# Attention scores moved from inside the gate to the expert tiles, and all DCT tiles of the next group into the gate

## The chip, the cores and the metric

The kernel runs on one core of one Trainium2 chip. The metric is the device time of one execution in microseconds (us). Engines are named TensorE (PE), VectorE (DVE), ScalarE (ACT), GpSimd (POOL) and SyncE (SP, which issues transfers).

## What is computed

64 audio signals of 80000 samples are cut into 157 frames of 512 samples. Everything is float32.

```
h = frames @ DCT.T                                   # per signal: 157 tokens x 512
x = layernorm(h)
key, query = exp(i*pi*tanh(x @ Wk)), exp(i*pi*tanh(x @ Wq))   # 4 sets x 8 planes
V = x @ Wv + bv
total = sum over sets and planes of Re(cumsum(key * V) * conj(query)), weighted
pos_contrib = the same with fixed positional phases
gate = sigmoid(x @ Wg + bg)
total = gate * total + (1 - gate) * pos_contrib
h = h + x + total / norm @ Wo + bo
x = layernorm(h)
scores = softmax(mean over tokens of x @ Wg_ffn + bg_ffn)     # 16 experts
e = argmax(scores)                                   # one expert per signal
h = h + scores[e] * (x @ We[e] + be[e])
```

The cumulative sums are computed as a causal matrix product: scores of query and key tokens, masked, then applied to V.

## The kernel before

The 64 signals are worked in 16 groups of 4. A group's 4 x 160 padded tokens make five tiles: four of 128 tokens (32 tokens of each of the 4 signals) numbered 0 to 3, and a tile called TAIL. The order of instructions is written out by hand; each engine works through its own list, and semaphores between engines are set from what each instruction reads and writes. TensorE's results go to PSUM through one pool of four buffers of two banks (`psum()`, L91), which every stage shares, so a stage may have to wait until an earlier result has been read out.

The main loop (L1218) does for each group g, after a special first group:

1. `project_and_values(g)` (L1085): query and key phases, V by seven products of half size (a Strassen-like scheme), and, for the group before, the turning of the normalised tokens (`x2T`), the choice of the expert (`route`, `pick`) and the fetch of its weights (`fetch`, four indirect transfers issued by POOL). Near its end stands `fold_twice(g+1, 0)`: DVE folds the first half of the next group's frames (`xT`) for the DCT.
2. `gate(g)` (L1133): seven gate products in the order 1, 6, 2, 7, 5, 4, 3 (`gate_product`, matmuls at L655), each followed by DVE sums of its result (L100) and ACT tanh operations (L672). Products 2, 4 and 3 go on adding in the buffers of products 1, 7 and 5. Between the products stand other steps: `fold_once` and `fold_twice(g+1, 1)` for the second half of the next frames, `scores(g)` and the DCT of the next group's tiles.
3. `experts_and_embedding(g)` (L1155): three of the five expert tiles of group g-1, the rest of the DCT tiles of group g+1, their layernorm factors, and the loads of group g+2's frames.
4. `attention(g)` (L1174): the scores are applied to V (`read`, L697), two more expert tiles (L1185, L1210) and the output products.

Group 15 has no next group: its gate does no DCT, and `experts_and_embedding` is left out. So `experts_and_embedding` runs for groups 1 to 14.

The steps that the change moves:

- `scores(g)` (L674): 20 matmuls of 32 columns each, L681, then two DVE operations (L682, L683) that make `att`, which `read` uses.
- `embed(g, n)` (L259) is the DCT of one tile: two matmuls at L270 and two at L272, on the folded frames. `embed_statistics` (L284) takes its result out of PSUM: two ACT copies (L292, L293), a DVE add and subtract (L294, L295), then layernorm moments on DVE (L232, L233). For tile 0 and 1 it needs the first half of the frames, for 2, 3 and TAIL the second half too.
- `embed_deviations` (L304): a few small POOL operations over the five tiles' moments; `embed_res` on ACT follows them.
- `expert(g, n)` (L960): 16 matmuls at L940 into the four 32-row strips of one buffer, one strip for each of the four signals with its own weights `we`; then `expert_out` (L948), one DVE operation (L951), and the stores to DRAM issued by SP.
- `add_bias(g, n)` (L931): one DVE operation (L934) per tile.
- `keep_deviations` and `spread_deviations` (L329, L337): the layernorm factors go to DRAM and come back to all partitions as `scale`, issued by SP; `scale_all` in `attention` uses them on DVE (L363).

Sums and differences on DVE that go through the helpers `add` and `sub` appear in the profile at L100 and L99, whoever calls them. A float32 matmul of the program is executed as two passes, so 16 expert matmuls appear as 32 in the profile.

Of the kernel before, what the change touches and what calls it, by code (L numbers as in the profile page):

```python
# [30 lines left out]
TAIL = NM - 1  # L31
# [22 lines left out]
def audio_tower(ctx: ExitStack, tc: tile.TileContext, a, out):  # L54
# [36 lines left out]
    def psum():  # L91

        return ps_mm.tile([P, 2, 512], F32, tag="mm", name="mm")

    def bank():
        return psum()[:, 0, :]
# [8 lines left out]
    def tile_of(x, n):  # L105
        return x[..., P * SLOT[n] : P * (SLOT[n] + 1)]
# [122 lines left out]
    def moments(mv, h):  # L229

        st = small.tile([P, 6], F32, tag="st", name="st", bufs=4)
        nc.vector.bn_stats(st, h)  # L232
        nc.vector.bn_aggr(mv, st)  # L233

    def deviation(rstd, var):

        nc.gpsimd.tensor_scalar(rstd, var, EPS, None, ALU.add)  # L237
        nc.gpsimd.tensor_tensor(rstd, rstd, power[:, : rstd.shape[-1]], ALU.pow)

    def shifts(mean, rstd):  # L240

        shift = small.tile([P, NM], F32, tag="shift", name="shift")[:, : rstd.shape[-1]]
        nc.gpsimd.tensor_tensor(shift, mean, rstd, ALU.mult)
        nc.gpsimd.tensor_scalar(shift, shift, -1.0, None, ALU.mult)  # L244
        return shift
# [13 lines left out]
    def embed(g, n):  # L259

        s = S[g]
        if n == 0:
            s["res"] = {}
            s["res2"] = []
        h = psum()
        h, odd = h[:, 0, :], h[:, 1, :].rearrange("p (n j) -> p n j", n=2)
        by_r = h.rearrange("p (j r) -> p r j", r=4)
        ft = tile_of(s["xT"], n)
        for i in range(2):
            nc.tensor.matmul(by_r[:, 2 * i, :], ft[:, 2 + i], dct_e[:, i, :], start=True, stop=True)  # L270
        for i in range(2):
            nc.tensor.matmul(odd[:, i, : P + 1], ft[:, i], trig_o[:, i, :], start=True, stop=True)  # L272
        s["h", n] = h, odd

    def residual(g, n):

        s = S[g]
        if n == TAIL:
            return p1.tile([P, D], F32, tag="res_t", name="res_t", bufs=3)
        if n % 2 == 0:  # L280
            s["res2"].append(p1.tile([P, 2, D], F32, tag="res", name="res", bufs=6))
        return s["res2"][-1][:, n % 2, :]

    def embed_statistics(g, n):  # L284
        s = S[g]
        if n == 0:
            s["mv"] = small.tile([P, NM, 2], F32, tag="mv", name="mv", bufs=2)
        h, odd = s.pop(("h", n))
        s["res"][n] = r = residual(g, n)
        of_r, to_r = (x.rearrange("p (j r) -> p r j", r=4) for x in (h, r))  # L290
        sines = p2.tile([P, P + 1], F32, tag="sines", name="sines")
        nc.scalar.copy(sines, odd[:, 1, : P + 1])  # L292
        nc.scalar.copy(to_r[:, 0::2, :], of_r[:, 0::2, :])  # L293
        add(to_r[:, 1, :], odd[:, 0, :P], sines[:, :P])  # L294
        sub(to_r[:, 3, :], odd[:, 0, 1 : P + 1], sines[:, 1 : P + 1])  # L295
        moments(s["mv"][:, SLOT[n], :], r)
# [7 lines left out]
    def embed_deviations(g, of=range(NM), known=False):  # L304

        s = S[g]
        lo, hi = min(SLOT[n] for n in of), max(SLOT[n] for n in of) + 1
        rstd, mv = deviations[g % 2][:, lo:hi], s["mv"][:, lo:hi]
        if not known:
            deviation(rstd, mv[:, :, 1])  # L310
        shift = shifts(mv[:, :, 0], rstd)
        more = small.tile([P, NM], F32, tag="more", name="more", bufs=6)[:, : hi - lo]
        nc.gpsimd.tensor_scalar(more, rstd, 1.0, None, ALU.add)  # L313
        for n in of:
            k = slice(SLOT[n] - lo, SLOT[n] - lo + 1)
            s["rstd", n] = rstd[:, k]
            s["st", n] = shift[:, k], more[:, k]
# [329 lines left out]
    def gate_product(g, i):  # L647

        s = S[g]
        if i == 1:  # L650
            s["gT"] = p1.tile([P, C, 2 * HN], F32, tag="gT", name="gT")
        (ps, first), rhs, w = room(g, i), operand(g, i), fac_g[i]
        for o in range(2):
            for c in range(2):
                nc.tensor.matmul(  # L655
                    ps[:, o, :HN],
                    w[:, c, o * P : (o + 1) * P],
                    rhs[:, c],
                    start=(first and c == 0),
                    stop=(c == 1),  # L660
                    skip_group_check=not first,
                )
        part = halves(s["gT"])
        if i != 2:
            gather(i, by_halves(ps), part)
        for k, m, n in ((2, 0, 0), (5, 1, 1), (3, 0, 1), (4, 1, 0)):
            if k == i:
                for o in range(2):
                    to = part[m][n][:, o]
                    c = 2 * n + o  # L670
                    of = ps[:, o, :HN] if i == 2 else to
                    nc.scalar.activation(to, of, AF.Tanh, bias=hbg[:, c : c + 1], scale=0.5)  # L672

    def scores(g):  # L674

        ps = bank()
        for n in range(NM):
            lo, hi = SEES[n]
            for i in range(GB):
                to = ps[Q * i : Q * (i + 1), START[n] : START[n] + hi - lo]  # L680
                nc.tensor.matmul(to, kf[:, SLOT[n], i], qf[:, lo // Q : hi // Q, i], start=True, stop=True)  # L681
        nc.vector.tensor_tensor(att[:, 0], ps[:, :NS], hmask, ALU.mult)  # L682
        nc.vector.tensor_tensor(att[:, 1], att[:, 0], share, ALU.add)  # L683
# [247 lines left out]
    def add_bias(g, n):  # L931

        s = S[g]
        nc.vector.scalar_tensor_tensor(s["res"][n], s["be"], s["gate"], s["res"][n], ALU.mult, ALU.add)  # L934

    def expert_chunk(g, n, c, ps):

        s = S[g]
        for i in range(GB):
            nc.tensor.matmul(  # L940
                ps[Q * i : Q * (i + 1), :],
                s["x2T"][:, c, i, Q * n : Q * (n + 1)],
                s["ws"][i][:, c, :],
                start=(c == 0),
                stop=(c == C - 1),
            )

    def expert_out(g, n, ps):  # L948
        s = S[g]
        o, at = s["res"][n], Q * BLOCK[n]  # L950
        nc.vector.scalar_tensor_tensor(o, ps, s["gate"], o, ALU.mult, ALU.add)  # L951
        for i in range(GB):

            for lo, hi in ((0, Q),) if n < TAIL else ((0, Q // 2), (Q // 2, LT)):
                queue = nc.sync if g + 1 < NG or i % 2 == 0 else nc.scalar
                if g + 2 == NG and n in ORDER[1:4]:
                    queue = nc.gpsimd
                queue.dma_start(out=out[GB * g + i, at + lo : at + hi, :], in_=o[Q * i + lo : Q * i + hi, :])

    def expert(g, n, between=lambda c: None):  # L960
        ps = psum()
        for c in range(C):
            between(c)
            expert_chunk(g, n, c, ps[:, 0, :])
        between(C)
        expert_out(g, n, ps[:, 0, :])
# [166 lines left out]
    def gate(g):  # L1133
        ahead = g + 1 < NG
        for i in (1, 6, 2, 7, 5, 4, 3):
            gate_product(g, i)
            if i == 1:
                pick_gate(g - 1)
                bias(g - 1)
                fold_once(g + 1, 1)  # L1140
                add_bv(g, 0, slice(H, D))
                add_bv(g, 1)
            elif i == 5:
                scores(g)
                fold_twice(g + 1, 1)
                if ahead:
                    embed(g + 1, 0)
                    embed_statistics(g + 1, 0)
            elif i == 4 and ahead:
                add_bias(g - 1, TAIL)  # L1150
                add_bias(g - 1, 0)
                embed(g + 1, 1)
                embed_statistics(g + 1, 1)

    def experts_and_embedding(g):  # L1155

        new = g + 1
        expert(g - 1, TAIL)
        for n in (2, 3, TAIL):
            embed(new, n)  # L1160
            embed_statistics(new, n)
        embed_deviations(new)
        load_half(g + 2, 0)
        load_half(g + 2, 1)
        for n in (1, 2, 3):
            add_bias(g - 1, n)
        for n in range(NM):
            embed_res(new, n)
        expert(g - 1, 0)
        keep_deviations(new)  # L1170
        expert(g - 1, 1)
        spread_deviations(new)
# [59 lines left out]
    g = NG - 1  # L1232
# [158 lines left out]
```

## Time and profile before

| | us |
|---|---|
| median of 3 runs | 1321.88 (1321.7 to 1322.51) |
| profiled execution, its own time | 1321.45 |
| its span | 1319.5 |
| TensorE busy | 1312.9 |
| VectorE busy | 1026.6 |
| GpSimd busy | 593.0 |
| ScalarE busy | 406.5 |

The span is the time from the first to the last instruction that the profile has of the program; the execution's own time lies around it. Busy time is the time in which an engine works on an instruction; matmul ends are modelled, so the starts of matmuls are the firmer numbers. "PEld" is the loading of a matmul's weights, which can overlap the matmuls before it. "PEldq" is an instruction that TensorE's sequencer runs itself, such as a wait for a semaphore. Lines named L... are lines of the kernel before.

### The profile page before, as it was taken

Reading aid. Unit: us, or ns where it says so; the run is one execution under the profiler, and the core shown is the slowest. Engines: PE = TensorE matmul, PEld = TensorE weight load, DVE = VectorE, ACT = ScalarE, POOL = GpSimd, SP = SyncE. Lnnn points to the kernel's source line nnn. Section 1 sums busy time; section 2 is a strip of 40 time slices with the busy share of each in tenths; the row PEclk is TensorE's granted clock in tenths of the full one; section 3 lists DMA queues with packets and bytes.
Section 4 is the critical chain, followed back from the end, with each engine's and each line's share of the span. In section 5 each row is a group of like instructions: output and inputs, shape, how many; then the busy total and the mean of one; then the engine's idle time right before and its main releaser. Section 6 shows DMA issues by size and latency. Waiting matters only on the chain.

```text
span 1319.5 us, 25282 instructions
## 1 busy us (share of the span) xinstructions
PE 1312.9 (99%) x9784; PEld 859.4 (65%) x9784; DVE 1026.6 (78%) x2074; ACT 406.5 (31%) x708; POOL 593.0 (45%) x748
## 2 busy tenths in 40 slices
PE   9999999999999999999999999999999999999998
PEld 6677665675756667576676656757566675766762
DVE  5888787787878878787787877878788787877683
ACT  2524233141332314233142331413333142331410
POOL 2356354344534355254443543445343552544314
PEclk9999999999999999999999999999999999999999
DMA  7015225152341524315152250523414243141506
GB/s 238 1 51 176 83 61 186 28 177 81 114 152 28 175 69 172 90 49 191 35 176 83 68 183 25 178 80 119 147 30 163 82 173 86 48 151 35 178 8 207
DMA packets 60575, 144.41 MB, mean 109 GB/s; under 512 B 14136, under 2 KB 31432, under 8 KB 52520
## 3 DMA queue, kind: packets, MB, share of 16 engines
q1 hardware_dynamic: 45620, 62.68, 17.1%
q0 software_dynamic: 14336, 79.47, 16.6%
q8 instruction: 78, 1.28, 0.4%
q10 hardware_dynamic: 500, 0.64, 0.2%
q14 instruction: 41, 0.34, 0.1%
HBM read 102.47 MB, written 20.62 MB: 93 GB/s over the span
## 4 chain that ended last, share of the span: by engine, by line
PE 97%; issue 1%; POOL 1%; DMA 1%; DVE 0%; POOLq 0%; DVEq 0%
PE mm L445 29%; PE mm L940 19%; PE mm L655 17%; PE mm L250 9%; PE mm L697 9%; PE mm L270 3%; PE mm L600 3%; PE mm L272 3%; PE mm L636 1%; PE mm L681 1%; PE mm L201 1%; DMA t_v<-in_we,rows 1%; PE mm L219 0%; PE mm L191 0%; PE mm L835 0%
## 5 line engine op out<-in xcount | busy, mean ns | idle before, releaser
L940 PE MATMUL mm<-we,x2T 128*32 128x512 f32 x2400 | 269.9, 595 | 0.0
L940 PEld LDWEIGHTS mm<-we,x2T 128*32 128x32 f32 x2400 | 72.0, 110 | 157.6 <-issue 154.8
L705 DVE TENSOR_TENSOR gT<-mm,gT 128x320 f32<-128x320 f32 x256 | 116.8, 487 | 37.2 <-PE mm L697 32.7
L237 POOL TENSOR_SCALAR rstd<-mv 128x2 f32<-128x2 f32 (+1 forms) x50 | 11.7, 235 | 257.2 <-DVE mv L233 257.1
L237 POOL TENSOR_SCALAR dev<-mv 128x5 f32<-128x5 f32 (+1 forms) x20 | 10.5, 525 | 239.3 <-DVE mv L233 238.7
L697 PEld LDWEIGHTS mm<-att,v 32*128 32x128 f32 x2048 | 94.9, 185 | 34.0 <-issue 12.6
L697 PE MATMUL mm<-att,v 32*128 32x320 f32 (+3 forms) x2048 | 114.6, 358 | 0.0
L515 POOL TENSOR_TENSOR v<-v,bv 128x512 f32<-128x512 f32 (+1 forms) x45 | 72.9, 1638 | 71.1 <-ACT v L464 71.0
L771 ACT ACTIVATE x<-res,shift,rstd 128x512 f32<-128x512 f32 x61 | 46.4, 807 | 184.1 <-POOL shift L244 172.2
L672 ACT ACTIVATE gT<-gT,hbg 128x320 f32<-128x320 f32 x90 | 45.7, 554 | 153.3 <-DVE gT L100 153.3
L232 DVE BATCH_NORM_STATS2 st<-res 128x6 f32<-128x512 f32 x128 | 87.8, 686 | 3.3
L951 DVE SCALAR_TENSOR_TENSOR res<-mm,gate,res 128x512 f32<-128x512 f32 x64 | 48.0, 749 | 54.1 <-PE mm L940 54.1
L327 POOL TENSOR_TENSOR res<-res,bo 128x512 f32<-128x512 f32 x64 | 80.6, 1291 | 13.1 <-ACT res L323 13.0
L445 PE MATMUL mm<-t_o,sum 128*128 128x256 f32 x384 | 85.5, 379 | 0.0
L445 PE MATMUL mm<-t_v,sum 128*128 128x256 f32 x360 | 80.1, 379 | 0.0
L445 PEld LDWEIGHTS mm<-t_o,sum 128*128 128x128 f32 x384 | 73.0, 190 | 9.9
L894 POOL DMA_INDIRECT we<-in_we,rows x60 | 60.3, 1006 | 34.3 <-DVE rows L890 20.3
L445 PEld LDWEIGHTS mm<-t_v,sum 128*128 128x128 f32 x360 | 68.4, 190 | 9.3
L323 ACT ACTIVATE res<-res,shift,more 128x512 f32<-128x512 f32 x64 | 46.9, 803 | 89.4 <-POOL more L313 89.4
L250 PE MATMUL mm<-wv,xT 128*128 128x512 f32 x160 | 71.8, 592 | 0.0
L100 DVE TENSOR_TENSOR res<-mm,res 128x512 f32<-128x512 f32 x64 | 43.4, 678 | 33.8 <-PE mm L445 17.4
L655 PE MATMUL mm<-sum,wg 128*128 128x320 f32 x240 | 69.5, 432 | 0.0
(219 smaller groups left out, 2807.9 us busy)
## 6 DMA issues: line engine op xcount, KB each, us to landing
xT<-in_frames SPq DMA_DIRECT2D x32, 640.0 KB
out<-res SPq DMA_DIRECT2D x236, 64.0 KB
x2T<-turned SPq DMA_DIRECT2D x150, 80.0 KB
x2T<-turned POOLq DMA_DIRECT2D x90, 80.0 KB, 2.8
scale<-row SPq DMA_DIRECT2D x15, 320.0 KB
out<-res_t SPq DMA_DIRECT2D x62, 32.0 KB
out<-res_t SPq DMA_DIRECT2D x62, 26.0 KB
wg<-in_wg SPq DMA_DIRECT2D x1, 1024.0 KB
```

The costliest lines, as they stand in the source:

```text
L232: nc.vector.bn_stats(st, h)
L250: nc.tensor.matmul(ps, tile_of(x[:, c], n), w[:, c, :], start=(c == 0), stop=(c == C - 1))
L323: nc.scalar.activation(s["res"][n], s["res"][n], AF.Identity, bias=shift, scale=more)
L327: nc.gpsimd.tensor_tensor(r, r, bo, ALU.add)
L445: nc.tensor.matmul(ps[:, b, :], lhs[:, c, P * b : P * (b + 1)], w[:, c, :], start=(first and c == 0), stop=(c == 1), skip_group_check=not ...
L515: nc.gpsimd.tensor_tensor(v, v, by, ALU.add)
L655: nc.tensor.matmul(ps[:, o, :HN], w[:, c, o * P : (o + 1) * P], rhs[:, c], start=(first and c == 0), stop=(c == 1), skip_group_check=not f ...
L697: nc.tensor.matmul(to, s["v", n][q, c * P : (c + 1) * P], by, start=(n == 3), stop=(n == TAIL))
L705: nc.vector.tensor_tensor(th, r[:, :, n], th, op)
L894: nc.gpsimd.indirect_dma_start(out=ws[b][:, n * k : n * (k + 1)], out_offset=None, in_=of, in_offset=bass.IndirectOffsetOnAxis(ap=rows[:, ...
L940: nc.tensor.matmul(ps[Q * i : Q * (i + 1), :], s["x2T"][:, c, i, Q * n : Q * (n + 1)], s["ws"][i][:, c, :], start=(c == 0), stop=(c == C - 1),
L951: nc.vector.scalar_tensor_tensor(o, ps, s["gate"], o, ALU.mult, ALU.add)
```

## The change

In the gate, the scores are no longer put after product 5, except in group 15. The DCT tiles stand elsewhere: tile 0 after product 6, tile 1 after product 2, tiles 2, 3 and TAIL after product 3, the last product. Before, tile 0 stood after product 5 (behind the scores), tile 1 after product 4, and tiles 2, 3 and TAIL behind the TAIL expert tile. `experts_and_embedding` now begins with the scores, then POOL's `embed_deviations`, the two bias additions of tiles TAIL and 0 that stood in the gate, and then the TAIL expert tile; what follows is as before. So TensorE's order at that place is: last product, DCT tiles 2, 3 and TAIL, scores, expert tiles TAIL, 0 and 1, read.

```diff
@@ gate(g)
                 fold_once(g + 1, 1)
                 add_bv(g, 0, slice(H, D))
                 add_bv(g, 1)
-            elif i == 5:
-                scores(g)
+            if i == 5:
+                if not ahead:
+                    scores(g)
                 fold_twice(g + 1, 1)
-                if ahead:
-                    embed(g + 1, 0)
-                    embed_statistics(g + 1, 0)
-            elif i == 4 and ahead:
-                add_bias(g - 1, TAIL)
-                add_bias(g - 1, 0)
-                embed(g + 1, 1)
-                embed_statistics(g + 1, 1)
+            for n in {6: (0,), 2: (1,), 3: (2, 3, TAIL)}.get(i, ()) if ahead else ():
+                embed(g + 1, n)
+                embed_statistics(g + 1, n)
 
     def experts_and_embedding(g):
 
         new = g + 1
+        scores(g)
+        embed_deviations(new)
+        add_bias(g - 1, TAIL)
+        add_bias(g - 1, 0)
         expert(g - 1, TAIL)
-        for n in (2, 3, TAIL):
-            embed(new, n)
-            embed_statistics(new, n)
-        embed_deviations(new)
         load_half(g + 2, 0)
         load_half(g + 2, 1)
```

## The prediction

> **What bounds the kernel.** First the page: span and busy times.
>
> ```profile
> span 1319.5 us, 25282 instructions
> PE 1312.9 (99%) x9784; PEld 859.4 (65%) x9784; DVE 1026.6 (78%) x2074; ACT 406.5 (31%) x708; POOL 593.0 (45%) x748
> PE 97%; issue 1%; POOL 1%; DMA 1%; DVE 0%; POOLq 0%; DVEq 0%
> ```
>
> TensorE (PE) is busy 99% and is 97% of the chain that ended last. So I look for what lies between PE's matmuls. In the timeline of PE, the gate of every group from 1 to 14 starts 80.06 us after the one before (673.21, then 753.26), to a hundredth; one group will do. The stretch that changes runs from its gate, 673.21, to its first read, 704.77: 31.57 us. Timeline of PE; start, length, group of equal matmuls:
>
> ```profile
> 684.07 1.03 PE L681 MATMUL mm<-qf,kf 128*32 128x128 f32 x40
> 685.03 0.71 PE L270 MATMUL mm<-dct_e,xT 128*128 128x128 f32 x4
> 685.58 0.61 PE L272 MATMUL mm<-trig_o,xT 128*128 128x129 f32 x4
> 686.03 2.32 PE L655 MATMUL mm<-xT,t_g 128*128 128x320 f32 x8
> 688.18 0.61 PE L270 MATMUL mm<-dct_e,xT 128*128 128x128 f32 x4
> 688.62 0.61 PE L272 MATMUL mm<-trig_o,xT 128*128 128x129 f32 x4
> 689.07 2.32 PE L655 MATMUL mm<-sum,wg 128*128 128x320 f32 x8
> 691.32 3.64 PE L940 MATMUL mm<-we,x2T 128*32 128x512 f32 x32
> 694.89 0.71 PE L270 MATMUL mm<-dct_e,xT 128*128 128x128 f32 x4
> ...
> 697.77 7.07 PE L940 MATMUL mm<-we,x2T 128*32 128x512 f32 x64
> 704.77 1.80 PE L697 MATMUL mm<-att,v 32*128 32x320 f32 x32
> ```
>
> 128*32 means four column strips, each with its own weights; 128*128 is the whole array. Start to start, a gate product costs 2.15 us (686.03 to 688.18), but 2.25 before an expert tile. A DCT tile costs 0.89 after a product (688.18 to 689.07), 1.00 after an expert tile, and 0.99 ahead of one. One expert tile costs 3.57, two together 7.00, so each more costs 3.43.
>
> Then the waits that PE's sequencer runs, by line; count, min/median/max in ns, first and last start. First answer: DCT line, 684 to 686 us. Second: expert line, 687 to 692. Third: expert line of the last group, 1271 to 1273.
>
> ```profile
> L270 PEldq EVENT_SEMAPHORE  x1: 51/51/51, 684.5 to 684.5; - x1
> L940 PEldq EVENT_SEMAPHORE  x10: 51/51/1133, 687.7 to 689.8; - x10
> L940 PEldq EVENT_SEMAPHORE  x9: 51/51/51, 1271.4 to 1272.3; - x9
> ```
>
> The first expert tile waits for the x2T transfers, four expert weights and a freed PSUM buffer: ten wait instructions before and between its first four matmuls. Nine that hold nobody up take 0.9 us, so about 0.11 each. In the second answer they are over 1.5 us before PE's expert matmuls start (691.32): hidden.
>
> **What the Trainium skill says.** "TensorEngine Tiling (Array Packing)", Key Properties: "Changing tiling mode (not just tile) drains the TensorE". The trace agrees; prices below. "TensorE: Matmul & The Clock Gate", LDWEIGHTS: a load takes its columns / 1.2 ns, so 107 ns for 128 columns (estimate). Leaving strips, the first full-width matmul takes 0.21 us to the next where 0.11 is usual, so one such load is laid bare. "Perfetto Trace Analysis", Sequencer Loop: matmuls are pushed into the engine's queue, control instructions are executed by the sequencer itself. The trace agrees: the DCT wait at 684.53 stands behind all 40 score matmuls, of which 20 had not started, so the sequencer leads by some 20 matmuls.
>
> **The change part by part** (hundredths that the views do not print are from the instruction records).
>
> Switches. Per group, before: scores in, scores out, TAIL expert in, out, experts 0 and 1 in, out. After: the scores and three expert tiles in once, out once. Removed: two entries, each 0.093 (last product matmul to next start 0.362 against 0.269) plus 0.023 for the slower first quad: 0.23. Leaving the expert tile: 0.113 + 0.10 = 0.22. Leaving the scores: their last quad starts at 684.884, a neighbour in the same mode could start 0.028 later, the DCT tile starts at 685.030: 0.118 + 0.10 = 0.22. Sum 0.67. That neighbours in strips cost nothing is seen at 1281.96, where an expert quad follows router strips (L845) at their own pace.
>
> The ten waits. They now stand behind score matmuls of 24 ns instead of products of 269. The wait that followed the scores before started 0.462 after the first score matmul, in every group; the first of the ten will too. At 0.106 to 0.126 each (four before the first matmul, then two before each of the next three) the fourth ends at +0.84, the tenth at +1.53. A matmul starts 0.055 after a wait that it depended on (1280.842 to 1280.898). So strip 0 starts at +0.89, strip 3 at +1.59, where seamless running gives +0.85 and +0.87. Strips run at their own pace (at 1295.4 three went on while the fourth waited), but strip 3 has 24 passes of 0.429 of its own and can't catch up. Lost: 0.72, and 0.025 for its cold first pair.
>
> Sum of the stretch after. Seven products and five DCT tiles, one entry: 19.63 to the scores. Strip 3: +1.61, 23 passes 9.87, last pass and exit 0.50 (697.77 to 704.77 has the same end). Total 31.62 against 31.57: +0.05 us a group, times 14 groups (1 to 14; first and last are untouched) = +0.7 us. The profiled execution took 1321.45 for a span of 1319.5; the median of the runs is 1321.88. I add the 0.7: **1322.6 us**.
>
> What is moved, and hidden. In us from the gate's start: DCT tiles 0 and 1 run at 4.3 and 7.4. Tile 0 needs VectorE's (DVE's) fold, done at 3.60 and 4.19; the matmuls that read these parts come at 4.75 and 4.97. Product 7 needs the buffer of product 6: free at 7.2, needed at 8.25. Tiles 2, 3, TAIL at 16.86, 17.75, 18.64 need the second fold, done about 15.4. Everything arrives. If the fold were late, PE would wait one to one.
>
> The evictions of the last three tiles then queue on DVE ahead of the attention scores' two operations: those end about 25.4, the read needs them at 31.6. add_bias TAIL and 0 follow, later than before, and TAIL's expert_out at about 27.5 instead of 22.5. SyncE (SP) thus issues TAIL's eight stores (3.23), then the two loads of the frames (1.28), then expert 0's stores, four row stores, expert 1's stores and the scale load 5 us later at its head, and 1.3 later at its end, since it worked without a gap from 704.2 before. The scale was issued at 709.3 and its packets were done by 712.4; DVE takes it up at 719.6. Cover about 6 us. The frames are wanted 40 us later. POOL's deviations come 4 us earlier. The expert weights landed by 18.1 in the worst group; their waits now come from 20.1 on instead of 14.5. No queue ends later at its end than it is needed.
>
> **The rivals.** (a) The waits stay hidden: the sequencer gets further ahead, or handles met waits faster at the queue's end. Then the 0.67 to 0.69 is kept: 14 x 0.69 = 9.7, so 1312.2. For it: in every place of this trace such waits are hidden. Against: nowhere do they follow matmuls this short; a lead of 20 is worth 0.39 us here, 5 us in products. Half hidden gives 1317.
>
> (b) One of the ten, the third, is not yet met. It asks for DVE's subtraction of DCT tile 2, which frees the PSUM buffer. Before that come product 3's sum (0.79 to 0.82), ScalarE's (ACT's) tanh pair (1.01), its two copies, and DVE's add and subtract. Taken from the same sequence at 690.7 to 693.1, it ends 0.68 to 0.70 after the first score matmul and is seen by the sequencer 0.04 later; the third wait would end at 0.73 by itself. Lateness is paid one to one, by the whole group of ten. If one more short ACT copy (0.25) came in ahead, 14 x 0.25 = 3.5: 1326.1. It is slower by the bound below from 0.14 late on. For it: there is no slack. Against: DVE and ACT are through with their earlier work 0.8 and 0.6 before that sum begins and ends.
>
> (c) The change doesn't reorder PE as written: excluded, the built program has scores, TAIL, 0, 1 in a row.
>
> **How the numbers follow.** What a measurement of this kernel can tell from no change is about 0.2%, 2.6 us. Waits laid bare, as summed: 0.58, range 1320 to 1324.5, from +-0.15 a group on the sequencer's lead and pace. Rival (a) whole or half: 0.25, nearly all faster. Rival (b): 0.17, slower. So faster 0.25, same 0.58, slower 0.17. Range: 1314 leaves out the lower half of (a), 1326.5 the upper third of (b): 1314 to 1326.5.
>
> **What would show it.** Group period 80.05 to 80.15 on PE. Scores then expert tiles in a row; a first quad of L940 with four starts 0.2 apart, and the first strip started 0.89 after the scores. Ten waits of L940, starting in mid-scores and lasting 1.1 us. If strips start together within 0.87, (a) holds and the period is 79.4. If one of the waits is over 0.1 us long, (b). Idle of PE ahead of L270 or L655 would contradict the folds; DVE waiting for the scale would contradict the DMA part.

## The result, and the profile after

The changed kernel takes 1322.41 us (median of 12 runs, 1321.98 to 1323.82) against 1321.8 us for the kernel before in the same comparison (12 runs, 1321.02 to 1324.38). The ratio is 1.0002, 95% interval 0.9994 to 1.001: no difference that these runs can tell. The prediction was 1322.6 us.

The head of the page after, with the lines that answer to those shown of before: span, busy times, shares of the chain that ended last.

```profile
span 1320.1 us, 25338 instructions
PE 1313.3 (99%) x9784; PEld 920.6 (70%) x9784; DVE 1038.4 (79%) x2074; ACT 404.0 (31%) x708; POOL 602.7 (46%) x748
PE 97%; issue 1%; DMA 1%; POOL 1%; SPq 0%; DVE 0%; POOLq 0%
```

PE bounds the kernel as before, at 99% of the span, and has the same 9784 matmul passes. What stands out is PEld: 920.6 us of weight loading, where it was 859.4. The number of loads has not changed. The groups of the page say whose loads these are. First the two lines of before for the expert tiles (line, engine, operation, tile, shape, count, then busy us, mean ns, and the idle time ahead of them):

```profile
L940 PE MATMUL mm<-we,x2T 128*32 128x512 f32 x2400 | 269.9, 595 | 0.0
L940 PEld LDWEIGHTS mm<-we,x2T 128*32 128x32 f32 x2400 | 72.0, 110 | 157.6 <-issue 154.8
```

The same two lines of after:

```profile
L940 PE MATMUL mm<-we,x2T 128*32 128x512 f32 x2400 | 276.3, 593 | 0.0
L940 PEld LDWEIGHTS mm<-we,x2T 128*32 128x32 f32 x2400 | 132.0, 109 | 109.3 <-issue 65.1
```

A pass and a load last what they lasted (593 and 109 ns, against 595 and 110), but the loads cover 60 us more of time, because busy time counts once what overlaps: four strips' loads used to overlap each other, and now they are spread out. That is the mark of strips that no longer start together. The timeline of PE shows where, in group 8 (start us, length, group of equal matmuls); the gate begins at 673.99, and the last product, the scores and the expert tiles follow:

```profile
688.70 2.32 PE L655 MATMUL mm<-sum,wg 128*128 128x320 f32 x8
690.85 0.61 PE L270 MATMUL mm<-dct_e,xT 128*128 128x128 f32 x4
...
693.08 0.61 PE L272 MATMUL mm<-trig_o,xT 128*128 128x129 f32 x4
693.62 1.03 PE L681 MATMUL mm<-qf,kf 128*32 128x128 f32 x40
694.51 11.16 PE L940 MATMUL mm<-we,x2T 128*32 128x512 f32 x96
705.60 1.67 PE L697 MATMUL mm<-att,v 32*128 32x320 f32 x25
```

The stretch from the gate to the read takes 31.61 us (673.99 to 705.60); it took 31.57 before. The three expert tiles take 11.09 of it (694.51 to 705.60), where three of them at the old pace in one piece would take 3.57 + 2 x 3.43 = 10.43. Counted on PE from the query and key matmuls (L600) of one group to those of the next, groups 1 to 14 take 80.113 us in the mean, against 80.056 before: 14 x 0.057 = 0.8 us. The span grew by 0.6.

The waits of that place, in two windows of the after kernel's trace: until the first expert matmul, and from it on (count, min/median/max in ns, first and last start):

```profile
L940 PEldq EVENT_SEMAPHORE  x4: 51/51/51, 694.1 to 694.4; - x4
L940 PEldq EVENT_SEMAPHORE  x6: 51/51/51, 694.5 to 695.1; - x6
```

Ten waits, each 51 ns: none waited for anything, and in none of the 14 groups did one last longer. (A wait that does wait shows it: in the same place the kernel before has one of 1133 ns.) By the instruction records they start at 694.083, 694.194, 694.300, 694.406, and then in pairs 0.23 us apart; the four strips start at 694.513, 694.745, 694.977 and 695.208, which is 0.89, 1.12, 1.36 and 1.59 after the first score matmul. Four waits, a strip, two waits, a strip, two, a strip, two, a strip.

### The profile page after: what moved, and what is told of

The parts are those of the page before. It is cut to its first block, busy times and chain, and to the rows that moved or that the text cites. A ratio compares the mean times of both kernels' runs of the same rounds, so it can differ in the third digit from the quotient of the medians.

```text
span 1320.1 us, 25338 instructions
## 1 busy us (share of the span) xinstructions
PE 1313.3 (99%) x9784; PEld 920.6 (70%) x9784; DVE 1038.4 (79%) x2074; ACT 404.0 (31%) x708; POOL 602.7 (46%) x748
## 4 chain that ended last, share of the span: by engine, by line
PE 97%; issue 1%; DMA 1%; POOL 1%; SPq 0%; DVE 0%; POOLq 0%
PE mm L445 29%; PE mm L940 20%; PE mm L655 17%; PE mm L250 9%; PE mm L697 9%; PE mm L600 3%; PE mm L270 3%; PE mm L272 3%; PE mm L636 1%; PE mm L681 1%; DMA tables<-in_table_sums 1%; DMA t_v<-in_we,rows 0%; PE mm L201 0%; PE mm L219 0%; PE mm L835 0%
## 5 line engine op out<-in xcount | busy, mean ns | idle before, releaser
L940 PE MATMUL mm<-we,x2T 128*32 128x512 f32 x2400 | 276.3, 593 | 0.0
L940 PEld LDWEIGHTS mm<-we,x2T 128*32 128x32 f32 x2400 | 132.0, 109 | 109.3 <-issue 65.1
L327 POOL TENSOR_TENSOR res<-res,bo 128x512 f32<-128x512 f32 x64 | 95.0, 1511 | 13.1 <-ACT res L323 13.0
L237 POOL TENSOR_SCALAR dev<-mv 128x5 f32<-128x5 f32 (+1 forms) x20 | 4.9, 244 | 182.4 <-DVE mv L233 181.8
L716 ACT COPY u<-mm 128x512 f32<-128x512 f32 x16 | 9.4, 585 | 203.2 <-PE mm L445 203.2
```

The lines of the kernel that those rows point to most:

```text
L327: nc.gpsimd.tensor_tensor(r, r, bo, ALU.add)
L940: nc.tensor.matmul(ps[Q * i : Q * (i + 1), :], s["x2T"][:, c, i, Q * n : Q * (n + 1)], s["ws"][i][:, c, :], start=(c == 0), stop=(c == C - 1),
```

## The experiments

Two questions are to be settled. Does putting the scores and the expert tiles together really save the 0.67 us that the switches of tiling mode were priced at? And is it the ten waits that take it back, or something else in the new order (the evictions of three DCT tiles in a row on DVE, or the transfers)? In all of them "the period" is the mean that was used above: from the query and key matmuls of one group to those of the next, groups 1 to 14, in the one execution that was profiled. Within an execution it varies from group to group by 0.12 us at most (by 0.01 in most kernels), where whole executions of one kernel differ by up to 3.8 us. All ratios are to the kernel before, which took 1321.9 us in these comparisons.

**The scores behind the TAIL tile.** The same neighbours in strips, but the waits stand behind DCT matmuls of the whole array again, not behind the short score matmuls:

```diff
@@ experts_and_embedding(g), against the changed kernel
-        scores(g)
         embed_deviations(new)
         add_bias(g - 1, TAIL)
         add_bias(g - 1, 0)
         expert(g - 1, TAIL)
+        scores(g)
```

> The changed kernel with the scores put behind the TAIL expert tile instead of ahead of it. The number of switches of the array and the operations of every engine are those of the changed kernel; only what stands ahead of the ten waits differs, 24 DCT passes of 0.11 us instead of 40 score passes of 0.02. Theory (waits laid bare): the waits are hidden again, strip 3 starts with strip 0, the stretch from the gate to the read falls from 31.61 to 30.9 us, the period to 79.4, the time to about 1312 (0.7% below before). Rival 1 (the switches were worth nothing): time as the changed kernel, 1322. Rival 2 (the bunched evictions on VectorE hold the experts' buffers): it stays at or above 1320, since VectorE's list is the same but for the place of the attention scores' two operations.

Measured: 1312.34 us (1311.8 to 1314.48, 5 runs), ratio 0.992 (0.9907 to 0.9934). The period is 79.388. The timeline of PE in this kernel, group 8, and the waits of its TAIL tile:

```profile
689.97 0.61 PE L272 MATMUL mm<-trig_o,xT 128*128 128x129 f32 x4
690.51 3.64 PE L940 MATMUL mm<-we,x2T 128*32 128x512 f32 x32
693.97 1.01 PE L681 MATMUL mm<-qf,kf 128*32 128x128 f32 x40
694.79 7.05 PE L940 MATMUL mm<-we,x2T 128*32 128x512 f32 x64
701.77 1.80 PE L697 MATMUL mm<-att,v 32*128 32x320 f32 x32
```

```profile
L940 PEldq EVENT_SEMAPHORE  x9: 51/51/51, 688.4 to 689.5; - x9
```

Nine waits, the last a whole microsecond before the tile's first matmul at 690.51: hidden. The tile takes 3.46 us up to the scores, and these take 0.83 up to the next tile. This is the full gain, 80.056 - 79.388 = 0.67 a group, for the same switches. The kernel differs from the changed one in one line's place, and by 0.725 us a group.

**The DCT tiles moved alone.** The scores stay behind product 5, as before:

```diff
@@ gate(g), against the changed kernel
             if i == 5:
-                if not ahead:
-                    scores(g)
+                scores(g)
@@ experts_and_embedding(g)
-        scores(g)
```

> Only the DCT tiles are moved into the gate; the scores stay behind product 5, as before. Theory: one entry into strips (0.12) and one way out of an expert tile (0.22) less than before, the ten waits hidden behind DCT passes: period 80.06 - 0.33 = 79.72, time about 1317.2. Rival 1 (switches worth nothing): 1321.8. Rival 2 (bunched evictions cost): 1321 or more.

Measured: 1316.56 us (1316.02 to 1317.56, 5 runs), ratio 0.995 (0.9937 to 0.9964); period 79.720. That is 0.336 under before, for one entry into strips and one exit (0.116 + 0.22), and 0.332 over the kernel above, for the scores' own entry and exit, now paid again. Its evictions of three DCT tiles in a row on DVE (the operations that take the results out of PSUM) are those of the changed kernel, and cost nothing visible: the waits are met, and the three expert tiles take 10.44 (693.04 to 703.48), which is the old pace.

```profile
L940 PEldq EVENT_SEMAPHORE  x9: 51/51/51, 691.0 to 691.9; - x9
693.04 10.51 PE L940 MATMUL mm<-we,x2T 128*32 128x512 f32 x96
703.48 1.80 PE L697 MATMUL mm<-att,v 32*128 32x320 f32 x32
```

**The scores moved alone.** The kernel before, with the scores behind the last product and ahead of the TAIL tile; all DCT tiles where they were:

```diff
@@ gate(g), against the kernel before
             elif i == 5:
-                scores(g)
+                if not ahead:
+                    scores(g)
                 fold_twice(g + 1, 1)
@@ experts_and_embedding(g)
+        scores(g)
         expert(g - 1, TAIL)
         for n in (2, 3, TAIL):
             embed(new, n)
```

> Only the scores are moved, ahead of the TAIL expert tile; the DCT tiles stand where they stood before. Theory: one entry (0.12) and the way out of the scores (0.22) less than before, the ten waits laid bare (+0.74): period 80.06 + 0.41 = 80.47, time about 1327.5, slower than before. Rival 1 (the waits cost nothing, the switches count): 79.72, about 1317.2. Rival 2 (bunched evictions): nothing is bunched here, so 1317 to 1322.

Measured: 1326.53 us (1325.08 to 1328.17, 15 runs), ratio 1.0032 (1.0025 to 1.004); period 80.348. The timeline of PE, and the waits of the tile:

```profile
692.16 1.03 PE L681 MATMUL mm<-qf,kf 128*32 128x128 f32 x40
693.01 4.22 PE L940 MATMUL mm<-we,x2T 128*32 128x512 f32 x32
697.17 0.71 PE L270 MATMUL mm<-dct_e,xT 128*128 128x128 f32 x4
```

```profile
L940 PEldq EVENT_SEMAPHORE  x9: 51/51/51, 692.6 to 693.5; - x9
```

One entry and one exit are saved (0.34), and the group is still 0.29 longer: 0.63 is laid bare. The tile takes 4.16 from its first matmul to the DCT tile, where it took 3.57. There are nine waits here, three of them before the first strip, so the loss is one wait (0.11) short of the 0.74 expected. No DCT tile is moved, and DVE's work around the tile is as before but for the scores' own two operations; the loss is there all the same. It goes with the scores ahead of the waits.

**The waits ahead.** The changed kernel, and in the gate, ahead of DCT tile 2, one small matmul that reads one column of `x2T` from each of the four signals that the expert tiles work on. No later step reads the columns that it writes. It takes over the waits for the transfers of `x2T`, at a place behind a product:

```diff
@@ embed(g, n), against the changed kernel
+        if n == 2 and g > 1:
+            nc.tensor.matmul(odd[:, 0, 200:204], ident, S[g - 2]["x2T"][:, 0, :, 0], start=True, stop=True)
         by_r = h.rearrange("p (j r) -> p r j", r=4)
```

> The changed kernel with one small matmul added ahead of DCT tile 2, which reads one column of each of the sixteen transferred blocks of x2T; its result is not used. It takes over the waits for these sixteen transfers, at a place where the sequencer leads by products of 0.27 us; two wait instructions are left ahead of the expert tile and none between its first matmuls. Theory: strips start together 0.85 after the scores, -0.74, and the added matmul costs two passes of 0.11: period about 79.6, time about 1315. Rival (it is not the number of waits but that VectorE's eviction of tile 2 comes late, or the array's switch): the time rises by the added matmul alone, 0.22 x 14 = 3 us, to 1325.

Measured: 1315.05 us (1314.53 to 1316.36, 5 runs), ratio 0.9941 (0.9928 to 0.9955); period 79.611. The order of scores and tiles is that of the changed kernel; only the place of the waits differs. Lines from L268 on stand two further down here (the scores are L683, the experts L942). Waits of the added matmul, and of the expert tile:

```profile
L268 PEldq EVENT_SEMAPHORE  x7: 51/51/51, 684.1 to 684.7; - x7
```

```profile
L942 PEldq EVENT_SEMAPHORE  x3: 51/51/51, 690.7 to 692.2; - x3
```

Seven waits are some 2.5 us before the added matmul starts. Two stand between scores and first expert matmul (the third, at 692.2, belongs to the next tile). The timeline of PE:

```profile
687.24 0.28 PE L268 MATMUL mm<-x2T,ident 128*128 128x4 f32 x2
...
690.24 1.03 PE L683 MATMUL mm<-qf,kf 128*32 128x128 f32 x40
691.09 10.49 PE L942 MATMUL mm<-we,x2T 128*32 128x512 f32 x96
701.50 1.80 PE L699 MATMUL mm<-att,v 32*128 32x320 f32 x32
```

The three tiles take 10.42 instead of 11.09, and the four strips start within 0.02 us of each other (0.851 to 0.871 after the first score matmul). The kernel gains 80.113 - 79.611 = 0.50 a group, after paying 0.22 for the added matmul (its period is that much over the first experiment's).

**Six waits instead of ten.** As the last kernel, but the added matmul reads from two of the four signals only:

```diff
@@ embed(g, n), against the kernel with the waits ahead
-            nc.tensor.matmul(odd[:, 0, 200:204], ident, S[g - 2]["x2T"][:, 0, :, 0], start=True, stop=True)
+            nc.tensor.matmul(odd[:, 0, 200:202], ident, S[g - 2]["x2T"][:, 0, :2, 0], start=True, stop=True)
```

> As the kernel with the waits ahead, but the small added matmul reads the transposed block of two of the four signals only, so six of the expert tile's waits stay behind the 40 score passes. Theory (waits laid bare set the loss, in proportion): the last strip starts some 0.25 to 0.3 us later than with all waits ahead, period about 79.9 us, time about 1319.3 us. Rival (any small matmul there does the same, or the loss is a threshold that needs all ten waits): period 79.61 us, time 1315 us.

Measured: 1320.95 us (1319.16 to 1322.91, 21 runs), ratio 0.9989 (0.9983 to 0.9996); period 79.903. The waits, of which six belong to this tile and the seventh, at 696.3, to the next:

```profile
L942 PEldq EVENT_SEMAPHORE  x7: 51/51/51, 694.8 to 696.3; - x7
```

The last strip starts 1.14 to 1.24 after the first score matmul, by group, against 0.871 with two waits left and 1.59 (up to 1.64) with ten. The period is 0.29 over that of the kernel before this one, which left two waits there: the loss grows with the waits. The period is as expected; the median is 1.65 us above the expected time. Runs of this kernel lie between 1319.16 and 1322.91; the profiled one is that of 1322.91, and it began the first group's query and key matmuls at 47.96 us, against 45.79 in the kernel with the waits ahead: 2.2 us were lost before the work in which the two differ. What the other runs lost, and where, was not recorded, so the excess of the median stays open.

**Four expert tiles in a row.** If switches are worth so much, one more can be saved: from the first experiment's kernel, the expert tile that stands between the reads goes up to the others.

```diff
@@ experts_and_embedding(g), against the first experiment
         expert(g - 1, 1)
+        expert(g - 1, 2)
@@ attention(g)
         for c in range(C):
             read(g, c)
-            if c == 1 and ahead and g > 0:
-                expert(g - 1, 2)
```

> As the kernel with the scores behind the TAIL tile, and the expert tile that stands between the reads moved up behind the second expert tile, so that four expert tiles stand in a row and the reads stand together. Theory (a switch saved is worth 0.2 us, but the reads lose the expert tile that covers VectorE's folds between them; where they stand together in the last group, 160 passes took 7.89 us against 7.28): period about 79.8 us, time about 1317 us, slower than the kernel that it is built on (1312.3 us). Rival (only switches count): period 79.15 us, time 1309 us.

Measured: 1317.8 us (1317.49 to 1318.48, 6 runs), ratio 0.9968 (0.9956 to 0.998), period 79.791: 0.40 us a group slower than the kernel it was made from. The four tiles save 0.14 (10.42 for the three behind the scores, against 6.98 + 3.57 = 10.55), and the reads, now one after another, take 7.82 where the two halves took 2 x 3.64 = 7.28. The first rows of the first two and of the next two reads on PE, and the DVE operations that take their results out, group 8:

```profile
705.91 1.80 PE L697 MATMUL mm<-att,v 32*128 32x320 f32 x32
709.45 1.96 PE L697 MATMUL mm<-att,v 32*128 32x320 f32 x26
707.92 3.79 DVE L705 TENSOR_TENSOR gT<-mm,gT 128x320 f32<-128x320 f32 x8 [1.11 <-PE mm L697]
711.86 3.79 DVE L705 TENSOR_TENSOR gT<-mm,gT 128x320 f32<-128x320 f32 x8 [0.16 <-PE mm L697]
```

DVE takes 3.79 for two reads, PE took 3.54 for the first two and 4.29 for the next two (709.45 to 713.74), which need the buffers that DVE empties; DVE worked almost without a pause. With an expert tile between the reads DVE had 3.57 us more. A switch saved is only worth it where the piece that moves did not give another engine the time it needed.

## Why the prediction was right

*The switches, 0.67.* Right. With the waits hidden, the first experiment gains 0.67 a group (80.056 to 79.388), and the DCT tiles alone give 0.336 of it, one entry and one exit. What the Trainium skill states in "TensorEngine Tiling (Array Packing)", Key Properties, that a change of mode drains TensorE, agrees, and is priced here: 0.33 to 0.34 for in and out together. The prediction put the extra 0.10 of an exit down to one weight load of 107 ns laid bare. That is not shown: the traces record a weight load of a DCT tile, 128 columns, at 186 to 192 ns, one starting 0.11 us after the other, and no run takes an exit apart. Only its price is measured.

*The ten waits, 0.72 + 0.025.* The 0.72 is right to the hundredth: the first wait came at +0.461 (predicted 0.462), the strips started at +0.89 to +1.59 (predicted 0.89 and 1.59). The 0.025 for a cold first pair did not show: from the last strip's start to the read takes 10.39 in the changed kernel and 10.40 in the one with the waits ahead. The whole loss, changed kernel against the first experiment, is 0.725. The Trainium skill states in "Perfetto Trace Analysis", Sequencer Loop, that control instructions are run by the sequencer itself, where matmuls go into the engine's queue, and the after trace agrees: behind the scores the sequencer reaches the first wait only when the score matmuls are already half through, and each wait costs it 0.106 to 0.126. Met waits stay hidden as long as the matmuls that are already queued ahead of them last longer than the waits do. By the instruction records of group 8, 17 to 20 passes had not started when the sequencer came to the first of these waits, in all eight kernels: a lead of 0.38 to 0.43 us behind the scores, 2.08 behind the DCT tiles in the first experiment, 3.66 in the kernel before. Ten waits take 1.1.

*The stretch, 31.62.* It took 31.61. In some groups a strip came 0.03 to 0.05 later still (last strip at up to +1.64), so the mean period is 80.113, against the sum's 80.056 + 0.05. The prediction's own parts do not quite give that sum: 0.745 lost less 0.67 saved is 0.075. Measured are 0.725 less 0.67, that is 0.057 by the periods.

*The profiled execution, plus 0.7.* The periods added 0.8. The span grew by 0.6, since the first group's query and key matmuls began 0.4 later (45.89 against 45.51) and what follows those of the last group took 0.5 less (103.5 against 104.0). Over the eight profiled executions these two pieces vary by 2.4 and 1.6 us, so neither can be put down to the change. That the span and the medians (0.6 each) came so near the 0.7 is in part luck. The period is not: its two terms, 0.67 and 0.725, were measured apart.

*Rival (a), waits hidden, 1312.2.* It did not happen in the changed kernel, but its time was right: with the waits really hidden the time is 1312.34. *Half hidden, 1317*, is near what six waits did: without the added matmul's 0.22 their period would be 79.68, and 14 x (80.113 - 79.68) = 6 us under the changed kernel is 1316.4.

*Rival (b), the third wait not met.* All ten waits lasted 51 ns, in every group. The DVE timeline of after has the subtraction of tile 2 that the third wait asks for:

```profile
693.86 0.40 DVE L99 TENSOR_TENSOR res<-mm,sines 128x128 f32<-128x128 f32 x1
```

It ended at 694.26, 0.64 after the first score matmul (predicted 0.68 to 0.70); the wait came at +0.68. So there was only 0.04 us to spare, and the rival was a near one. In the kernel with the scores alone moved it came true once: in group 12 the third wait lasted 123 ns, and that group was the longest (80.447, against a mean of 80.348).

*What was hidden.* It stayed so. The fold for DCT tile 0 held a wait in PE's sequencer for 3.2 us (the longest of the four waits of DCT matmuls in group 8), and no matmul came later for it:

```profile
L270 PEldq EVENT_SEMAPHORE  x4: 51/212/3195, 673.6 to 690.3; - x4
```

The wait was over at 676.77, 1.5 us before the tile's matmul at 678.30. The attention scores' DVE operations ended 25.65 after the gate's start (predicted 25.4; needed at 31.61). The scale load was issued at 714.35, that is 40.4 after the gate's start instead of 36.1, and DVE took it up at 720.45, directly behind three sums and differences of the reads' results and without a pause: the later load held up nobody.

*What was not tried.* No run leaves the waits out altogether, since the matmuls could then read data that have not arrived. So the cost of one wait, 0.106 to 0.126, is read from the spacing; that nine cost 0.63 and ten 0.725 agrees with it.

## What to carry to other kernels

Waits that are already met still cost TensorE's sequencer some 0.11 us each. Here it was 17 to 20 passes ahead of the array when it came to them, so they were free where those passes last longer than all the waits together (2.08 us of DCT passes against 1.1), and bare where they do not (0.4 us of score passes). Put the consumer with the most new dependences behind longer matmuls, and the short ones after it. Here that is one line's place, and it turns a change worth nothing into 9.6 us (1312.34 against 1321.9), the best of all kernels run. When work in the same tiling mode is brought together, count both the switch saved and what the moved piece used to cover.

## What else the traces show of the hardware

Strips that start apart stay apart, as the prediction had counted on. In the changed kernel the second passes follow 0.429 after each strip's own first (694.513 to 694.942, 694.745 to 695.173), so strip 0 runs its second pass at 694.942 before strip 3 has begun its first at 695.208, and the 0.70 us between the first and the last strip is still there after 24 passes each: the read comes 11.98 after the first score matmul, where it comes after 11.27 when the strips start together. A late strip costs its whole lateness, though the other three have gone on. The passes of different strips do not keep the order in which they are issued either: strip 0's second load starts at 694.515, ahead of the two waits of strip 1 (694.532 and 694.638), but its second pass starts at 694.942, after strip 1's first at 694.745.

What had not been expected: executions differ by some 2 us before the work has settled. The first group's query and key matmuls began at 45.51 us before and 45.89 after, and at 47.85, 46.90, 45.53, 45.79, 47.96 and 45.73 in the profiled executions of the experiments, in the order told, though no edit touches what comes before them. From there to group 1's all eight took 49.16. For differences below 2 us the period is a better measure than the time.
